# Router on plain normalised rows, and B's and C's products on both halves of the array's rows

## The chip, the cores and the metric

The kernel runs on one core of a Trainium2 chip. The metric is the device time of one execution in microseconds (us), as the median of several runs; the profiles are single executions taken by the hardware profiler. TensorE (PE) multiplies matrices, ScalarE (ACT), VectorE (DVE) and GpSimd (POOL) do the elementwise work, and SyncE (SP) issues the DMA transfers. PE reads from SBUF and writes to PSUM, which has eight banks.

## What is computed

The input is 8 sequences of 512 tokens with 128 features. Four blocks follow one another, each with a layer norm in front and a residual sum behind: a state-space mixer, a mixture of eight experts, a local attention with 16 heads, and the same mixture of experts again.

```python
x = x + mixer(_layernorm(x))
x = x + experts(_layernorm(x))
x = x + attention(_layernorm(x))
x = x + experts(_layernorm(x))
```

The change touches two places in it. In the mixer, after a short convolution gives `xb` (64 channels), one matrix of 24 rows gives three things:

```python
proj = jnp.einsum('blc,oc->blo', xb, W_xproj)
dt_raw = proj[..., :DTRANK]                       # 8 rows
b_raw = proj[..., DTRANK:DTRANK + DSTATE]         # 8 rows
c_raw = proj[..., DTRANK + DSTATE:]               # 8 rows
delta = jnp.clip(jax.nn.softplus(jnp.einsum('blr,cr->blc', dt_raw, W_dt) + b_dt), 0.0001, 1.0)
b_term = jnp.tanh(b_raw)
c_term = jnp.tanh(c_raw)
```

In the mixture of experts two small matrices (128 x 8 each) give the router's weights; every expert is computed for every token:

```python
router_probs = jax.nn.softmax(jnp.einsum('bsh,he->bse', x, w_router), axis=-1)
gate_weights = jax.nn.softmax(jnp.einsum('bsh,he->bse', x, w_gating) / GATE_TEMP, axis=-1)
g = jnp.einsum('bsh,ehf->ebsf', x, w_gate)
u = jnp.einsum('bsh,ehf->ebsf', x, w_up)
h = jax.nn.silu(g) * u
expert_out = jnp.einsum('ebsf,efh->ebsh', h, w_down)
cw = router_probs * gate_weights
```

## The kernel before

**The bulk of the work.** The experts' three products dominate. Weights and activations are kept as two halves, a rounded high half and the rest as the low half, and each product is three matmuls (high by high, low by high, high by low: `matmul3`, line 467), in the type `fp32r`. `ffn_stream` (line 1081) walks over the two expert blocks, the 8 sequences, the 8 experts and 4 slices of 128 hidden features, and issues a gate product `g`, an up product `u` and, some slices later, the down product `y`. In between, `hidden` (line 1162) runs on the other engines: silu on ACT, the product with `u` on DVE, the high half of `h` on ACT or DVE, the low half on POOL or DVE. The first sequence's first four experts are done in two halves of 256 tokens, so that the stream can begin before the mixer of sequence 0 has ended.

**The side work.** The mixer of the next sequences, the attention, the layer norms and the routers are written as Python generators ("lanes"). A planner (`Clock` and `Lanes`, lines 120 to 352) keeps a model clock for each engine, with a cost per operation (for PE in `product`, line 136), and at each step of the stream lets those lanes issue whose inputs would be there by that clock. The result is one fixed order of instructions for each engine: the engines run it in order and wait on semaphores. A changed cost or a changed operation early in the program therefore moves instructions everywhere behind it. Side work may hold at most 4 of the 8 PSUM banks once the stream runs (`sides`, line 404).

**Layer norm and halves.** `normalised` (line 515) is used by the mixer, the attention and the experts. `layernorm` makes the normalised rows `xn` (tokens on partitions, one buffer, which is a lane resource called "ln"). PE transposes them into a PSUM bank `tp`, ACT copies that to the high half `hi` (rounded), DVE subtracts to give the low half `lo`. "ln" is given back as soon as the transposes are issued.

**The router.** `ffn_prep` (line 980) calls `normalised` for a sequence (or for a half of sequence 0) and then multiplies the two router matrices (32 columns, `wr`) with both halves, read as plain fp32: for each half and for each of the four blocks of 128 tokens one matmul, which writes to its own 32 partitions of the bank `lps`. Lines 1001 to 1006. It appears in the profile as `lps_f<-xt_f,route`. What follows is small work on DVE, ACT, POOL and two PE transposes.

**dt, B and C.** `mamba_front` (line 604), for sequences 1 to 7, computes `xb` into the partitions 0 to 63 and once more into 64 to 127. The dt product (`wdt`, W_dt times the dt rows) takes the first 256 tokens through the rows 0 to 63 of the array and the last 256 through the rows 64 to 127, into two banks `mde`. B's and C's product is in `rows_bc` (line 654): one fp32 matmul with all 128 rows and 512 tokens, into a third bank `mbc`; the rows 64 to 127 of its weights `wbc` are zeros. The weights' 32 columns are repeated four times (line 585). Then ACT takes tanh of the bank to `bc` (rounded), tanh of the partitions 32 to 63 in place, and DVE subtracts to give the rounding's rest in these partitions. For sequence 0, `half` (line 685) does the same for each half of the tokens with 256 columns: first B's and C's product on all 128 rows, then dt's on one half of the rows. A program of filler products (`warm`) keeps PE running in the first 40 us.

An fp32 matmul appears in the profile as two PE records, an fp32r matmul as one.

## Time and profile before

| what | value |
|---|---|
| median of the 3 runs shown | 1381.18 us (1379.3 to 1381.27) |
| profiled execution, its own time | 1383.66 us |
| its span, first to last instruction | 1381.9 us |
| mean granted TensorE clock | 0.985 |
| PE busy, records | 1340.0 us, 10330 |
| DVE busy | 1041.4 us |
| ACT busy | 957.3 us |
| POOL busy | 942.5 us |
| the experts' three products on PE | 455.7, 455.6 and 450.1 us, 1584 records each |
| the router's product on PE | 11.6 us, 256 records |
| B's and C's product on PE | 9.7 us, 18 records |
| dt's product on PE | 7.0 us, 32 records |

A line of the profile names the engine, the operation, the tile that is written and those that are read, the shape, a count, and times; "idle before" with an arrow names what the engine waited for. Nearly all instructions are recorded under line 259, because a helper issues them, so they are told apart by their tiles. Groups of PE overlap in time: matmuls are pipelined, so a group's busy time is more than what it adds to the stream, and the distance between the starts of two groups that follow without a pause is what one costs.

### The profile page before, as it was taken

The page shows a single profiled execution, that of the slowest core. Times are in us where ns is not written, and L with a number is a line of the kernel's source. Part 1 is how long each engine was busy: PE and PEld are TensorE (multiplying, and loading weights), DVE is VectorE, ACT ScalarE, POOL GpSimd, SP SyncE. Part 2 cuts the span into 40 slices and gives each one's busy share as a digit, 9 for nine tenths or more (in the row PEclk, how much of TensorE's full clock was granted, in tenths as well). Part 3 has the DMA queues.
Part 4 walks back from the last instruction along what each step waited for, and adds up shares of the span by engine and source line. Part 5 has one row for each costly group of instructions (what it writes and reads, how often), then busy time and mean ns, then how long its engine had stood idle before and what let it go on. Part 6 is the DMA issues. An engine that isn't in the chain of part 4 may idle for free. (4 is left out here: it accounts for less than half of the span.)

```text
span 1381.9 us, 29693 instructions
## 1 busy us (share of the span) xinstructions
PE 1340.0 (97%) x10330; PEld 1058.3 (77%) x10330; DVE 1041.4 (75%) x3137; ACT 957.3 (69%) x1674; POOL 942.5 (68%) x1057
## 2 busy tenths in 40 slices
PE   7779999999999999999999999999999999999997
PEld 6667777777878877777777777777777777778786
DVE  6877888888888567878888788678787787774443
ACT  7558577776775557776786877767767768775654
POOL 4656676667667577767676758666666666777776
PEclk8889999999999999999999999999999999999999
DMA  3221123223221322343435444443534333413111
GB/s 124 73 64 49 53 54 88 57 62 92 62 62 39 71 65 56 78 103 87 107 86 117 99 94 96 95 101 77 125 97 96 81 92 72 102 36 89 40 39 38
DMA packets 230846, 107.75 MB, mean 78 GB/s; under 512 B 86402, under 2 KB 226601, under 8 KB 230697
## 3 DMA queue, kind: packets, MB, share of 16 engines
q1 hardware_dynamic: 230696, 105.87, 32.6%
q8 instruction: 81, 1.33, 0.4%
q14 instruction: 69, 0.56, 0.1%
HBM read 77.64 MB, written 27.79 MB: 76 GB/s over the span
## 5 line engine op out<-in xcount | busy, mean ns | idle before, releaser
L259 POOL TENSOR_TENSOR h<-h,h 128x512 fp32r<-128x512 f32 (+1 forms) x512 | 644.5, 1269 | 295.1 <-ACT h L259 232.0
L259 PE MATMUL u<-xt_f,wu 128*128 128x512 f32 (+1 forms) x1584 | 455.7, 396 | 9.5 <-ACT h L259 5.8
L259 PE MATMUL g<-xt_f,wg 128*128 128x512 f32 (+1 forms) x1584 | 455.6, 396 | 4.7 <-DVE mst L259 2.6
L259 PE MATMUL y<-h,wd 128*128 128x512 f32 (+1 forms) x1584 | 450.1, 394 | 3.2 <-POOL h L259 1.7
L259 DVE TENSOR_TENSOR h<-u,h 128x512 f32<-128x512 f32 (+1 forms) x438 | 292.9, 674 | 169.5 <-PE u L259 109.5
L259 ACT ACTIVATE h<-g 128x512 f32<-128x512 f32 (+1 forms) x528 | 305.5, 584 | 140.7 <-PE g L259 116.6
L259 ACT CAST h<-h 128x512 fp32r<-128x512 f32 (+1 forms) x447 | 267.6, 605 | 190.3 <-DVE h L259 188.9
L259 PEld LDWEIGHTS u<-xt_f,wu 128*128 128x128 f32 x1584 | 289.6, 190 | 79.8 <-ACT h L259 7.9
L259 PEld LDWEIGHTS g<-xt_f,wg 128*128 128x128 f32 x1584 | 290.4, 191 | 73.3 <-issue 3.9
L259 PEld LDWEIGHTS y<-h,wd 128*128 128x128 f32 x1584 | 290.7, 190 | 71.6 <-POOL h L259 2.4
L259 POOL TENSOR_TENSOR acc<-acc,cwb 128x512 f32<-128x512 f32 (+1 forms) x115 | 147.6, 1284 | 52.1 <-DVE cwb L259 28.8
L259 ACT ACT_TABLE_LOAD x112 | 143.7, 1283 | 31.2 <-PE g L259 29.7
L259 DVE CUSTOM_DVE_ANT_0 amasked<-as,maskq 128x60 f32<-128x60 f32 x640 | 95.3, 214 | 5.1 <-PE as L259 4.7
L259 DVE TENSOR_TENSOR cwb<-y,cwb 128x512 f32<-128x512 f32 (+1 forms) x115 | 77.3, 672 | 21.1 <-PE y L259 11.0
L259 DVE TENSOR_TENSOR apt<-aw,maskk 125x400 f32<-125x400 f32 (+2 forms) x160 | 87.9, 574 | 0.1
L259 DVE SCALAR_TENSOR_TENSOR h<-h,g 128x512 f32<-128x512 f32 (+1 forms) x90 | 58.2, 651 | 39.5 <-ACT h L259 38.4
L259 ACT ACTIVATE apt<-apt 125x400 f32<-125x400 f32 (+2 forms) x160 | 80.5, 541 | 0.4
L259 DVE SCALAR_TENSOR_TENSOR h<-u,h 128x512 f32<-128x512 f32 (+1 forms) x90 | 58.3, 653 | 4.0
L259 DVE DVE_READ_ACCUMULATOR2_ANT amx<- 128x1 f32 x640 | 52.9, 83 | 0.0
L259 DVE CAST h<-h 128x512 fp32r<-128x512 f32 (+1 forms) x81 | 46.4, 579 | 1.4
L259 PEld LDWEIGHTS ao<-apt,v 125*32 125x32 f32 (+2 forms) x1280 | 27.4, 109 | 14.7 <-issue 6.6
L259 DVE COPY v<-avr 125x128 f32<-125x128 f32 (+2 forms) x40 | 24.0, 600 | 17.7 <-PE ao L259 17.3
(195 smaller groups left out, 1234.0 us busy)
## 6 DMA issues: line engine op xcount, KB each, us to landing
cwb<-cwd_f SPq DMA_DIRECT2D x124, 256.0 KB
aqd<-apc SPq DMA_DIRECT2D x32, 192.0 KB
ks<-aqd SPq DMA_DIRECT2D x48, 93.8 KB
x_fo<-x SPq DMA_DIRECT2D x16, 256.0 KB
aqd<-apc SPq DMA_DIRECT2D x32, 128.0 KB
x_f<-x SPq DMA_DIRECT2D x15, 256.0 KB
qs<-aqd SPq DMA_DIRECT2D x48, 75.0 KB
aod<-aos SPq DMA_DIRECT2D x24, 100.0 KB
```

The costliest lines, as they stand in the source:

```text
L259: f(*args, **kw)
```

## The change

The router now reads the normalised rows as they are. `normalised` gets a switch `plain`, with which ACT copies the transposed rows a second time, unrounded, over the buffer `xn`, and `ffn_prep` multiplies that with one matmul for each block of 128 tokens. The buffer "ln" is given back after the router's products, no longer after the transposes, and the bank `tp` after both ACT's copy and DVE's subtraction.

B's and C's product for sequences 1 to 7 is split like dt's: 64 rows for each half of the tokens, into the second half of the same bank that holds dt's product of these tokens. So there are two banks `mde` and none `mbc`; tanh and subtraction come in two pieces each, and the banks are given back by the step that makes `delta`. `rows_bc` is gone. The weights `wbc` are written to both halves of the rows. For sequence 0, B's and C's product uses the rows 0 to 63 and dt's the rows 64 to 127, for both halves of the tokens.

```diff
-    def normalised(xc, tag, halves, nt=NT, give=True, quick=False):
+    def normalised(xc, tag, halves, nt=NT, give=True, quick=False, plain=False):
...
             e = pe.transpose(tp[:, t * P : (t + 1) * P], xn[:, t, :], ident)
-        lanes.give("ln", e)
+        if not plain:
+            lanes.give("ln", e)
         yield "A"
         hi, lo = halves()
         tp = tp[:, : nt * P]
-        act.copy(hi, tp)
+        e = act.copy(hi, tp)
+        if plain:
+            xn = xn.rearrange("p t d -> p (t d)")[:, : nt * P]
+            e = act.copy(xn, tp)
         yield "V"
-        freed(dve.tensor_tensor(lo, tp, hi.bitcast(F32), ALU.subtract))
+        freed(max(e, dve.tensor_tensor(lo, tp, hi.bitcast(F32), ALU.subtract)))
         yield "T"
-        return hi, lo
+        return (hi, lo, xn) if plain else (hi, lo)
...
-        pool.tensor_copy(
-            wbc.rearrange("p (c n) -> p c n", c=4), pa[:, None, A_PBC : A_PBC + 32].to_broadcast([P, 4, 32])
-        )
+        for h in range(2):
+            pool.tensor_copy(
+                wbc[INNER * h : INNER * h + INNER].rearrange("p (c n) -> p c n", c=4),
+                pa[:INNER, None, A_PBC : A_PBC + 32].to_broadcast([INNER, 4, 32]),
+            )
...
-        pde = yield from sides(*(([P, L // 2], f"mde{b}_{h}") for h in range(2)))
+        both = yield from sides(*(([P, 2, HALF], f"mde{b}_{h}") for h in range(2)))
+        for j, w in enumerate(("wdt", "wbc")):
+            for h in range(2):
+                hs = slice(INNER * h, INNER * h + INNER)
+                pe.matmul(both[h][:, j], consts[w][hs], xb[hs, h * HALF : (h + 1) * HALF], start=True, stop=True)
+        pde = [t[:, 0] for t in both]
+        yield "A"
+
+        bc = sb.tile([P, L], F32R, tag="bc", name=f"mbc{b}")
         for h in range(2):
-            hs = slice(INNER * h, INNER * h + INNER)
-            pe.matmul(pde[h], consts["wdt"][hs], xb[hs, h * L // 2 : (h + 1) * L // 2], start=True, stop=True)
-        bc, bc_there = yield from rows_bc(b, sb, consts, xb, L, second_act=lambda: act.activation(zb, v, AF.Silu))
+            act.activation(bc[:, h * HALF : (h + 1) * HALF], both[h][:, 1], AF.Tanh)
+        for h in range(2):
+            act.activation(both[h][32:64, 1], both[h][32:64, 1], AF.Tanh)
+        act.activation(zb, v, AF.Silu)
+        yield "V"
+        for h in range(2):
+            low = bc[32:64, h * HALF : (h + 1) * HALF]
+            bc_there = dve.tensor_tensor(low, both[h][32:64, 1], low.bitcast(F32), ALU.subtract)
         yield "V"
...
-    def rows_bc(b, sb, consts, xb, n, second_act=None, c=0):
...
-            pe.matmul(pbc, consts["wbc"], xb, start=True, stop=True)
-            pe.matmul(pde, consts["wdt"][hs], xb[hs], start=True, stop=True)
+            pe.matmul(pbc, consts["wbc"][:INNER], xb[:INNER], start=True, stop=True)
+            pe.matmul(pde, consts["wdt"][INNER:], xb[INNER:], start=True, stop=True)
...
-        xt = yield from normalised(xc, nm, halves, nt, t0 + nt == NT, quick=nt < NT)
+        *_, xf = yield from normalised(xc, nm, halves, nt, t0 + nt == NT, quick=nt < NT, plain=True)
...
-        for i in range(2):
-            for t in range(nt):
-                pe.matmul(
-                    lps[32 * t : 32 * t + 32], wr, xt[i][:, t * P : (t + 1) * P].bitcast(F32),
-                    start=(i == 0), stop=(i == 1),
-                )
+        for t in range(nt):
+            e = pe.matmul(lps[32 * t : 32 * t + 32], wr, xf[:, t * P : (t + 1) * P], start=True, stop=True)
+        lanes.give("ln", e)
```

More of the change, by code (lines that the diff above doesn't have):

```diff
@@ L652, in mamba_front @@
         handed[b] = xb, zb, delta, bc, bc_there, clock.end["A"] + LAGS["A"]
-    def rows_bc(b, sb, consts, xb, n, second_act=None, c=0):
-        pbc = (yield from side([P, L], f"mbc{b}_{c}"))[:, :n]
-        pe.matmul(pbc, consts["wbc"], xb, start=True, stop=True)
-        yield "A"
-        bc = sb.tile([P, L], F32R, tag="bc", name=f"mbc{b}_{c}")[:, :n]
-        act.activation(bc, pbc, AF.Tanh)
-        act.activation(pbc[32:64], pbc[32:64], AF.Tanh)
-        if second_act:
-            second_act()
-        yield "V"
-        there = freed(dve.tensor_tensor(bc[32:64], pbc[32:64], bc[32:64].bitcast(F32), ALU.subtract))
-        return bc, there
     def spread(dst, consts, bc, i, m):
@@ L706, in half @@
             pde, pbc = yield from sides(([P, HALF], f"mde0_{c}"), ([P, L], f"mbc0_{c}"))
-            hs = slice(INNER * c, INNER * c + INNER)
             pbc = pbc[:, :HALF]
-            pe.matmul(pbc, consts["wbc"], xb, start=True, stop=True)
-            pe.matmul(pde, consts["wdt"][hs], xb[hs], start=True, stop=True)
+            pe.matmul(pbc, consts["wbc"][:INNER], xb[:INNER], start=True, stop=True)
+            pe.matmul(pde, consts["wdt"][INNER:], xb[INNER:], start=True, stop=True)
             add[c](scanned(c, pbc, pde))
```

## The prediction

> **What bounds the kernel now.** I read the busy times by engine first. TensorE's row stands alone:

> ```profile
> PE 1340.0 (97%) x10330; PEld 1058.3 (77%) x10330; DVE 1041.4 (75%) x3137; ACT 957.3 (69%) x1674; POOL 942.5 (68%) x1057
> ```

> 97% is an average over stages, so the table by stretch comes next (columns: the stretch, its length, then busy us of PE, weight loads, DVE, ACT and POOL with their instruction counts, the granted clock, the DMA share, GB/s):

> ```profile
> 0.00:45.00 45.00, 33.31 (x188) 28.18 (x189) 30.87 (x65) 25.07 (x54) 20.98 (x28) 0.83 0.37 112
> 45.00:70.00 25.00, 21.02 (x131) 18.29 (x133) 18.94 (x57) 16.67 (x41) 17.93 (x28) 0.89 0.26 70
> 70.00:450.00 380.00, 365.69 (x1784) 291.80 (x1783) 316.46 (x603) 270.14 (x466) 254.09 (x264) 0.98 0.24 62
> 450.00:1200.00 750.00, 745.24 (x7269) 581.48 (x7268) 584.94 (x2222) 535.59 (x930) 517.44 (x619) 1.00 0.41 91
> 1200.00:1370.00 170.00, 170.00 (x944) 135.40 (x944) 87.71 (x189) 108.18 (x183) 127.03 (x117) 1.00 0.22 52
> ```

> Length minus PE's column is PE's idle time: 11.7 us in the first 45, 4.0 in the next 25, 14.3 up to 450, 4.8 up to 1200, none up to 1370. From 450 on PE's stream alone sets the time; before 450 it mostly does, with 30 us of waits; in the first 45 us a dependent chain through all engines does. So the change is priced in PE time first, and ACT, which receives work, is watched before 450 us. A PE group's cost in the stream is the distance from its start to the next group's start, since PE's ends are modelled.

> **The router.** The change takes its product from 16 PE records per sequence (two halves, four column groups, two records each) to 8. The timeline of PE shows both sizes: the usual 16, and, in the sequence near 1147 us where the second half came late, 8 by themselves:

> ```profile
> 1147.89 0.43 PE L259 MATMUL lps_f<-xt_f,route 128*32 128x128 f32 x8 [0.30 <-DVE xt_f L259]
> 1148.25 0.50 PE L259 MATMUL g<-xt_f,wg 128*128 128x512 f32 x1
> ...
> 1225.08 0.65 PE L259 MATMUL lps_f<-xt_f,route 128*32 128x128 f32 x16
> 1225.65 0.97 PE L259 MATMUL u<-xt_f,wu 128*128 128x512 f32 x3
> ```

> 16 records take 1225.65 - 1225.08 = 0.57 us, 8 take 0.36. That saves 0.21 us, in 15 full sequences and the second half of the first one (whose two column groups run beside each other, so as many waves go): 16 x 0.21 = 3.4 us. The first half's lies in the head.

> **B and C.** Per sequence from the second on (7), dt's product is 4 records of 64 rows and B/C's is 2 records of 128 rows x 512:

> ```profile
> 119.03 0.70 PE L259 MATMUL mde<-mxb,wdt 64*128 64x256 f32 x4
> 119.66 0.97 PE L259 MATMUL u<-xt_f,wu 128*128 128x512 f32 x3
> 120.46 1.02 PE L259 MATMUL mbc<-mxb,wbc 128*128 128x512 f32 x2
> 121.32 0.60 PE L259 MATMUL tp_f<-ident,xn_f 128*128 128x128 f32 x4
> ```

> dt costs 119.66 - 119.03 = 0.63 us, B/C 121.32 - 120.46 = 0.86 us, 0.43 per record. After, B/C is four more 64-row records on 256 columns, two in each row half, behind dt's. Half the columns is half of 0.43 per record, so two records in each half, the halves beside each other, cost 2 x 0.215 = 0.43 us. Upper end: they cost what dt's four cost with their switch of form, 0.63. Less than 0.43 is excluded, because the records of one half follow each other. I take 0.43, because the router's row shows added waves at their streaming price (0.21 for two of 128 columns). Saved: 0.86 - 0.43 = 0.43 each (lower end 0.23), x 7 = 3.0 us (1.6).

> **The head.** For the first half of sequence 0, dt's product stands behind B/C's on PE, 15.30 to 16.52 us, and DVE waits 2.49 us for it; B/C's subtraction, whose tanh was done at 16.17, queues behind that and starts at 17.08. With both products in different row halves dt is done about 1.1 us earlier. The planner puts 7 filler products instead of 5 in front of the next needed one (0.25 us each by the 1.23 us for 5), so 0.5 us remains, and ACT's wait of 1.78 us for the second half's B/C passes it on. Later, at 41.24, PE waits 2.36 us for DVE's low half; then the router's remaining 4 records (0.57) and three gate products (0.81) run. After, the router needs only ACT's new copy, and two of the three gate products need only the high half; both fit into that wait. Up to 0.57 + 0.54 less, but the next product needs DVE's 41.11 + 0.67 = 41.78, so 0.8 at most, and DVE, busy from 36.9 to 46 with short pauses, takes back part. I take 0.5 + 0.5 = 1.0 us for the head; ends 0 and 1.3.

> **What is added.** Router: one ACT copy of 128x512 from PSUM per sequence, 0.58 us as the cast beside it (mean 558 ns over 17 with two halves of 0.37): 15 x 0.58 + 2 x 0.37 = 9.4 us. B/C: two tanh become four, 4 x 0.38 (0.76 for two of 256 at 15.41) against 1.19 for two of 512 (at 69.99): 0.33 x 7 = 2.3 us. So 11.8 us more on ACT. DVE's subtraction of 0.68 becomes two of 0.42: 1.1 us. POOL copies B/C's weights as two halves instead of one of 0.287 us at 6.2, 8 us before use. No DMA is added (SP issues the same number); SP's queue sees some loads change places. Cover: ACT is idle 110 us between 70 and 450 and 214 between 450 and 1200. If the cover is gone the price is 11.8 us, at the lower end nothing. I take nothing, because PE's waits on ACT in the whole run are few:

> ```profile
> PE u L259 <- ACT h L259: 5.8, 3, 4.5
> PE mbx L259 <- DVE mst L259: 4.3, 2, 2.4
> PE g L259 <- DVE mst L259: 2.6, 1, 2.6
> ```

> (us, times, longest). The new wait of the router on ACT's copy has the expert stream queued behind it on PE; in the built order the router's products stand where they stood, after the low half's place, so by then the copy (ahead of the low half's subtraction) has been issued. The layer-norm buffer is held until the router's product, 3 to 8 us longer; once, near 184 us, a mixer's layer norm starts in that gap and comes 4 us later; dt's product of that front stands at 219.56. One PSUM bank per front is saved.

> [...]

> **Sum.** 3.4 + 3.0 + 1.0 = 7.4 us. The profiled execution's own time is 1383.66 us (span 1381.9); it becomes 1376.3. The median of the runs shown is 1381.18, 2.5 us less, so 1373.8. With the lower ends (1.6, head 0) 5.0 us: 1376.2; with head 1.3: 1373.5. The planner's clock sees the new costs and reorders everything after some 55 us, so waits before 450 move by a few us either way: own range 1371 to 1377.

> **Rivals.**
> 1. ACT takes the pace (slower). Place: the queue of ACT before `h`, where the copies and tanh stand. Price: all 11.8 us, gain 7.4: +4.4, 1385.6. It is slower by 0.2% when (7.4 + 2.8) / 11.8 = 86% of the added ACT time turns up as PE waits. For it: between 77 and 82 us PE stops 4.53 us behind ACT's table load and exponentials. Against: ACT's idle time, and after 450 PE waits only 4.8 us for anything.
> 2. The gain before 450 is eaten, because the next wait there ends when it ended before. Left: 10 routers after 450, 2.1 us: 1379.1. For it: 30 us of PE waits there. Against: they are few and long (9.5 of them between 77 and 92 us), and PE stood still for the router in only two of its 17 places (at 41.24 and 1147 us).
> 3. The new order shortens those waits of 77 to 92 us. In the built order two weight casts move ahead of that place on ACT, and DVE multiplies the first `h` before the last scan, not behind it. Half gone: 1373.8 - 4.8 = 1369.0.
> 4. It does not do what it says: the row halves do not overlap. Then 8 records of 0.215 and the switch (0.63 - 0.43 = 0.20) make 1.92 us against 1.49: 3.0 us lost instead of won, 3.4 + 1.0 - 3.0 = 1.4, 1379.8. Against: dt's four records, 0.63 us for what would be 0.86 in series.

> **The numbers.** Forecast 0.60, rival 1 0.10, rival 2 0.17, rival 3 0.10, rival 4 0.03. Within 0.2% (about what a measurement of this kernel can tell from no change) is 1378.4 to 1383.9: rivals 2 and 4 mostly, 0.19. Faster: forecast, rival 3 and a little of 2, 0.71. Slower: rival 1, 0.10. The range from 1368 to 1381 leaves out rival 1 and the edges.

> **What would show it.** In the profile after: the router in 8 records, 0.36 us to the next start; dt and B/C as one group of 8 records within 1.06 us (1.26 at the upper end, 1.92 for rival 4); the first gate product starting before 41 us; PE busy less by about 6 us; PE's waits behind ACT still near 6 us. The forecast is wrong if PE's waits between 45 and 450 us, 18.3 us now, grow by more than 4, and rival 3 holds if they shrink by as much.

## The result, and the profile after

The changed kernel takes 1399.7 us (median of 4 runs, 1395.56 to 1400.78), the kernel before 1380.24 us in the runs beside it: ratio 1.0135, interval 1.0112 to 1.0159. It is slower by 19 us where 7 us less was forecast. The profiled execution took 1400.08 us, its span is 1398.3 us.

First the busy times by engine, then the table by stretch of the kernel after (columns as in the prediction; the last stretch of 170 us, with no idle time in either, is left out):

```profile
PE 1344.8 (96%) x10218; PEld 1058.9 (76%) x10218; DVE 1049.5 (75%) x3133; ACT 969.9 (69%) x1728; POOL 941.1 (67%) x1052
```

```profile
0.00:45.00 45.00, 33.52 (x189) 29.36 (x190) 31.66 (x67) 25.34 (x55) 21.24 (x29) 0.84 0.37 112
45.00:70.00 25.00, 19.39 (x119) 16.68 (x118) 16.12 (x51) 15.41 (x37) 16.33 (x26) 0.91 0.27 78
70.00:450.00 380.00, 357.32 (x1681) 281.06 (x1680) 293.70 (x572) 264.29 (x479) 246.19 (x255) 0.97 0.22 58
450.00:1200.00 750.00, 743.23 (x7184) 580.23 (x7183) 607.21 (x2242) 543.75 (x953) 513.79 (x610) 1.00 0.43 92
```

PE has 112 records fewer and yet is busy 4.8 us longer, and between 45 and 450 us it is idle 5.6 + 22.7 = 28.3 us where it was 18.3. The forecast named its own refutation there (waits growing by more than 4). The added ACT time is as forecast (969.9 - 957.3 = 12.6 us), and DVE is not busier between 70 and 450 us but less busy, by 22.8 us: it stands still more, and 22.3 us of its work have moved behind 450 us.

The new products, in PE's timeline of the kernel after:

```profile
129.07 0.43 PE L259 MATMUL lps_f<-xn_f,route 128*32 128x128 f32 x8
129.42 0.97 PE L259 MATMUL g<-xt_f,wg 128*128 128x512 f32 x3
...
204.46 0.70 PE L259 MATMUL mde<-mxb,wdt 64*128 64x256 f32 x4
204.99 0.60 PE L259 MATMUL mde<-mxb,wbc 64*128 64x256 f32 x4
205.52 0.73 PE L259 MATMUL y<-h,wd 128*128 128x512 f32 x2
```

From start to next start the router costs 129.42 - 129.07 = 0.35 us, dt and B/C together 205.52 - 204.46 = 1.06 us. Both are the forecast's prices. So the loss is not in PE's products that were changed.

To see where it comes, I set the starts of the gate products (`g`, 1584 records in both) side by side. The first one starts 1.0 us earlier than before. The 481st, 437.0 us before, starts 12.0 us later (449.0), but there the side work is not level: the mixer's last spread product follows at 442.9 us before, and only at 490.9 after. The 553rd starts 16.6 us later, with the same mixer products behind it in both, and the end is 16.4 us later. I call the 553rd **the mark**: it splits the run into the stage that holds the mixers of later sequences, and the rest. Its line before, then after:

```profile
489.80 0.62 PE L259 MATMUL g<-xt_f,wg 128*128 128x512 f32 x2
```

```profile
506.36 0.63 PE L259 MATMUL g<-xt_f,wg 128*128 128x512 f32 x2
```

So the whole loss lies before the mark; from there to the end both kernels take the same (892.1 and 891.9 us). The two profiles are 16.4 us apart where the medians are 19.5, since the profiled execution of before took 1383.66 us.

What PE waits for between 45 and 450 us in the kernel after, costliest first, and DVE's waits between 45 and 460 us for the mixer's spread products, again after:

```profile
PE g L259 <- DVE mst L259: 4.7, 2, 4.5
PE u L259 <- ACT h L259: 4.1, 5, 2.1
PE u L259 <- DVE mst L259: 2.9, 3, 2.2
```

```profile
DVE mbx L259 <- PE mbx L259: 10.3, 12, 1.7
DVE mcc L259 <- PE mcc L259: 7.8, 7, 2.6
```

Before, DVE waited 3.4 us for `mbx` and 0.5 us for `mcc`:

```profile
DVE mbx L259 <- PE mbx L259: 3.4, 7, 1.0
DVE mcc L259 <- PE mcc L259: 0.5, 1, 0.5
```

With `macc`'s the sum of these waits is 4.4 us before and 20.2 us after: PE waits for DVE's scans `mst`, and DVE waits for PE's products of the mixer. One such place in the timeline of all engines, after:

```profile
152.17 1.21 DVE L259 TENSOR_TENSOR_SCAN mst<-mdec,mbx 128x512 f32<-128x512 f32 x1
...
153.43 1.62 PE L259 MATMUL u<-xt_f,wu 128*128 128x512 f32 x3 [2.20 <-DVE mst L259]
...
155.27 1.48 PE L259 MATMUL y<-h,wd 128*128 128x512 f32 x3
155.51 0.69 DVE L259 TENSOR_TENSOR macc<-mcc,mst 128x512 f32<-128x512 f32 x1 [1.76 <-PE mcc L259]
...
157.42 0.40 PE L259 MATMUL mbx<-mbc,sel 128*128 128x512 f32 x1
...
157.86 0.70 DVE L259 TENSOR_TENSOR mbx<-mbx,mxb 128x512 f32<-128x512 f32 x1 [1.66 <-PE mbx L259]
...
159.06 0.69 DVE L259 TENSOR_TENSOR h<-u,h 128x512 f32<-128x512 f32 x1
...
159.78 0.62 ACT L259 CAST h<-h 128x512 fp32r<-128x512 f32 x1 [6.42 <-DVE h L259]
159.80 0.96 PE L259 MATMUL g<-xt_f,wg 128*128 128x512 f32 x3 [1.28 <-DVE h L259]
```

PE stands 2.20 us for a bank that DVE's scan at 152.17 frees. Behind that in its queue stand the products `mcc` (154.85) and `mbx`, so DVE stands 1.76 us and 1.66 us for them. Behind its own `mbx` steps stands `h` (159.06), whose `u`, a product that started at 146.87, and whose silu, from 151.79 on, had long been there: ACT waits 6.42 us for it, and PE, 1.28 us, for the bank that it frees. Each engine works its queue in the program's order and holds what the other needs next. A second thing shows: the three `y` products at 155.27 take 1.48 us, where three at 149.67 take 0.86. The granted clock stands at 0.50 from 153.50 to 156.91 us. The stretch from 150 to 250 us before, then after:

```profile
150.00:250.00 100.00, 97.16 (x450) 75.63 (x450) 85.17 (x161) 70.55 (x114) 64.84 (x63) 1.00 0.28 74
```

```profile
150.00:250.00 100.00, 90.29 (x388) 69.32 (x387) 72.44 (x139) 61.94 (x110) 58.63 (x60) 0.95 0.22 60
```

6.9 us more idle, and 0.05 x 100 = 5 us lost at a lower granted clock. Over windows of 1 us from 45 to 250 us, the clock's shortfall sums to 15.0 us after and 9.6 us before. So by these windows 10.0 us of waits and 5.4 us of clock came on top. From the first gate product to the mark, from start to start, the kernel after takes 17.5 us more: 10.0 us of waits, 4.9 us of clock, and 2.6 us more for the products themselves at full clock, where the changed ones should have saved some 4. That the unchanged products cost several us more in the new sequence is measured; why, I have not found.

That is the trace's account. Whether the new order or the added work makes it had to be tried.

### The profile page after: what moved, and what is told of

It reads as the page before. It is cut to its first block, busy times and chain, and to the rows that moved or that the text cites. A ratio compares the mean times of both kernels' runs of the same rounds, so it can differ in the third digit from the quotient of the medians.

```text
span 1398.3 us, 29541 instructions
## 1 busy us (share of the span) xinstructions
PE 1344.8 (96%) x10218; PEld 1058.9 (76%) x10218; DVE 1049.5 (75%) x3133; ACT 969.9 (69%) x1728; POOL 941.1 (67%) x1052
## 5 line engine op out<-in xcount | busy, mean ns | idle before, releaser
L259 POOL TENSOR_TENSOR h<-h,h 128x512 fp32r<-128x512 f32 (+1 forms) x506 | 642.2, 1279 | 280.2 <-ACT h L259 216.5
L259 PE MATMUL g<-xt_f,wg 128*128 128x512 f32 (+1 forms) x1584 | 457.4, 397 | 12.0 <-DVE mst L259 6.7
L259 PE MATMUL u<-xt_f,wu 128*128 128x512 f32 (+1 forms) x1584 | 457.0, 397 | 11.4 <-ACT h L259 4.1
L259 PE MATMUL y<-h,wd 128*128 128x512 f32 (+1 forms) x1584 | 451.7, 395 | 4.7 <-POOL h L259 2.7
L259 DVE TENSOR_TENSOR h<-u,h 128x512 f32<-128x512 f32 (+1 forms) x430 | 286.6, 673 | 168.4 <-PE u L259 111.4
L259 ACT ACTIVATE h<-g 128x512 f32<-128x512 f32 (+1 forms) x528 | 305.4, 583 | 143.6 <-PE g L259 103.4
L259 ACT CAST h<-h 128x512 fp32r<-128x512 f32 (+1 forms) x455 | 272.3, 605 | 189.6 <-DVE h L259 188.5
L259 PEld LDWEIGHTS u<-xt_f,wu 128*128 128x128 f32 x1584 | 291.8, 191 | 83.7 <-ACT h L259 9.5
L259 PEld LDWEIGHTS g<-xt_f,wg 128*128 128x128 f32 x1584 | 290.3, 191 | 84.1 <-DVE mst L259 7.8
L259 PEld LDWEIGHTS y<-h,wd 128*128 128x128 f32 x1584 | 290.9, 190 | 74.7 <-POOL h L259 3.8
L259 POOL TENSOR_TENSOR acc<-acc,cwb 128x512 f32<-128x512 f32 (+1 forms) x115 | 146.8, 1276 | 65.4 <-DVE cwb L259 46.0
L259 DVE CUSTOM_DVE_ANT_0 amasked<-as,maskq 128x60 f32<-128x60 f32 x640 | 95.3, 214 | 5.8 <-PE as L259 5.8
L259 DVE SCALAR_TENSOR_TENSOR h<-h,g 128x512 f32<-128x512 f32 (+1 forms) x98 | 63.8, 654 | 42.1 <-ACT h L259 41.2
L259 DVE TENSOR_TENSOR cwb<-y,cwb 128x512 f32<-128x512 f32 (+1 forms) x115 | 77.4, 673 | 15.8 <-PE y L259 9.0
L259 DVE TENSOR_TENSOR apt<-aw,maskk 125x400 f32<-125x400 f32 (+2 forms) x160 | 88.6, 573 | 0.0
L259 ACT ACTIVATE apt<-apt 125x400 f32<-125x400 f32 (+2 forms) x160 | 81.7, 541 | 0.4
L259 DVE SCALAR_TENSOR_TENSOR h<-u,h 128x512 f32<-128x512 f32 (+1 forms) x98 | 63.9, 655 | 3.9
L259 DVE DVE_READ_ACCUMULATOR2_ANT amx<- 128x1 f32 x640 | 52.8, 82 | 0.0
L259 DVE CAST h<-h 128x512 fp32r<-128x512 f32 (+1 forms) x73 | 45.0, 618 | 1.2
L259 PEld LDWEIGHTS ao<-apt,v 125*32 125x32 f32 (+2 forms) x1280 | 27.5, 110 | 15.2 <-issue 7.8
L259 DVE COPY v<-avr 125x128 f32<-125x128 f32 (+2 forms) x40 | 27.4, 685 | 14.3 <-PE ao L259 14.0
```

What stands on the lines that cost most here:

```text
L259: f(*args, **kw)
```

## The experiments

Two devices recur. The planner decides the order by its own clock, so an edit that should not move anything charges that clock with the old call and issues the new one past it (`ghost` charges and issues nothing, `nc.` issues and charges nothing). And a constant of the planner changed by one or two thousandths of a us (a null change) gives another order of the same operations; the planner then also gives some steps to another engine (ACT's busy time is 957.3 us in before and 965.0 in n1, the first of them), so each engine's share is not quite the same.

**1. Is it the work or the order?** `e1_old_order` does all the change's work in the order of before (abridged):

```diff
+            nc.scalar.copy(xf, tp)                    # beside act.copy(hi, tp)
+        for t in range(nt):
+            nc.tensor.matmul(lps[...], wr, xf[...], start=True, stop=True)
-                pe.matmul(lps[...], wr, xt[i][...], ...)
+                pe.ghost("matmul", lps[...], wr, xt[i][...])
```

and the same for B and C. Its plain rows have a buffer of their own, so the layer norm's buffer is not held longer, as it is in the change. `e4_new_order` is its opposite: the order of after with the old products (`pe.ghost` for the new ones, no copy of the plain rows).

> All instructions of the change, in the order of the kernel before: the planner's clock is charged as if the old products, the old tanh pair and the old subtraction were issued, so every other instruction of the five engines stands where it stood before. The plain rows have a buffer of their own (the router's copied logits share it), and the small dt matrix lies in a buffer of xb to make room. Theory 'order' (the loss is the price of the changed order of all instructions, the changed instructions themselves do what the prediction priced): 1380.2 - 7.4 = about 1373 us, 1371 to 1377. Theory 'work' (the 11.8 us more on ACT, the split tanh and the new waits hold up the stream, in whatever order): 1390 us or more.

> The order of the changed kernel on every engine, with the products of the kernel before: the router on both halves in 16 records, no copy of the plain rows, B and C on all 128 rows (tanh still in four pieces). 'Order' (the 19 us are the new order's) says the time stays near the changed kernel's 1399.7 us or a little above it, since the dearer products return some 6.5 us to TensorE: 1396 to 1408. 'Work' (the added copies, tanh pieces and waits cost it) says about 1381, the time before.

Measured: e1 1380.78 us, ratio 0.9995 (0.998 to 1.0009); e4 1405.92 us, ratio 1.0174 (1.0149 to 1.0198). The whole 19 us follow the order, and 'work' is refuted twice. But e1 is not 1373 either, and misses 'order's 1371 to 1377: with nothing moved, the saving of 7 us does not arrive. In the order of after it does in part: e4, with the old products, is slower than after by some 5 us (by the ratios, interval about 1 to 10).

Where it went shows when e1's PE records are put beside before's one by one (the order is the same). The replaced groups give 6.9 us, which is the forecast's 7.4 nearly whole. PE's waits take back 2.3, and 2.4 are products that ran slower. The other 2.2 us stand in these two profiles, whose spans are 2.3 us apart (1379.6 and 1381.9), and not in the medians. The lead over before is 7.0 us at the gate product that before starts at 976.6 us, and 1.7 at 1189.8. PE at the place where most of it goes, e1's timeline and its stretches:

```profile
1142.58 0.43 PE L1033 MATMUL lps_f<-xf_f,route 128*32 128x128 f32 x8 [1.27 <-ACT xf_f L539]
```

```profile
1139.00:1143.00 4.00, 2.73 (x89) 1.96 (x87) 2.82 (x6) 3.97 (x8) 3.40 (x3) 1.00 0.49 55
1143.00:1147.00 4.00, 3.99 (x47) 2.80 (x47) 4.00 (x38) 3.80 (x6) 0.61 (x3) 0.63 0.10 32
1147.00:1151.00 4.00, 4.00 (x12) 2.98 (x11) 2.38 (x9) 1.53 (x4) 1.47 (x6) 0.51 0.66 120
```

and the same place before:

```profile
1143.00:1147.00 4.00, 3.25 (x84) 2.49 (x83) 3.32 (x6) 3.97 (x8) 3.40 (x4) 1.00 0.38 80
1147.00:1151.00 4.00, 3.37 (x61) 2.10 (x62) 3.85 (x37) 3.10 (x6) 0.94 (x2) 1.00 0.17 47
```

Before waits there as long, but in two pieces (0.91 and 0.30 us), and keeps its clock. In e1 one wait of 1.27 us is followed by 7 us at half speed, 3.4 us lost. So the saving is real in the products and was handed back where PE, earlier now, waits for what did not become earlier (here ACT's new copy). The clock's toll comes on top at this place; over the whole stream it is nearly level (12.3 us lost in e1, 11.5 in before), since e1 lost less before 450 us.

**2. One part at a time, planner live, and a null change.** `e2_router_alone` and `e3_bc_alone` take one half of the diff each. `n1_act` is the kernel before with

```diff
-            c = 0.1 + n / 1180
+            c = 0.102 + n / 1180
```

> The router's part alone, B and C as before, with the planner free to reorder. 'Work': 9.4 of the 11.8 us of added ACT time stand here, so most of the loss, 1394 to 1400 us. 'Order': the order moves nearly as much as with both parts (2841 of the lines of PE's order differ, with both parts 3042), so it can land anywhere from 1376 to 1400 us; near 1377 would say that this order is a good one.

> B's and C's part alone, the router as before, with the planner free. 'Work': 2.3 of 11.8 us of added ACT time against 3 us of saved PE time: 1380 us, within 3. 'Order': PE's order differs in only 649 lines, so a small move of either sign about 1377 us, 1373 to 1385.

> The kernel before with one number of the planner's clock changed: an ACT operation is charged 0.102 us fixed, not 0.100. No instruction is added or removed by the change itself, but the order changes (2782 lines of PE's differ), and with it some choices between two engines. 'Work': 1380 us, within 3. 'Order', in the form that the order before is better than its neighbours: 1385 to 1400 us. 'Order', in the form that just this change makes a bad order: 1380 us.

Measured: e2 1385.1 us (1.0025, 1.0014 to 1.0037), e3 1381.88 (1.0011, 0.9996 to 1.0026), n1 1388.63 (1.0066, 1.004 to 1.0091). Neither half costs 19 us, the two do not add up, and a change of no work at all costs 8 us. 'Work' fails on e2 and n1; e3 lies inside what both theories said and decides nothing.

**3. Is it a draw?** More changes of the planner's prices alone, in both kernels: `n2_before_dve` (DVE's fixed price 0.077 for 0.075), `n3_before_pe` (fp32r product 0.004 for 0.003), and on the changed kernel `a1_after_act`, `a2_after_dve` and `a4_after_priced`:

```diff
-            return n * 0.00053, "beside"
+            return n * (0.00084 if n > P else 0.00041), "beside"     # a4
```

> The changed kernel with the planner's fixed price of a ScalarE instruction at 0.102 instead of 0.100 us: the same work in another order (as with the kernel before, where this cost 8 us). 'Draw' (each order's waits are a draw, and the change only drew a bad one) says it leaves 1399.7 by several us, anywhere from 1378 to 1398. 'Worse as a kind' (the change leaves the planner a worse set of orders) says 1395 to 1405.

> The kernel before with the planner's fixed price of a VectorE instruction at 0.077 instead of 0.075 us: the same work in another order. 'Draw' (an order's waits are a draw, with a spread of some 10 us either way) says anywhere from 1374 to 1400. 'Settled' (the kernel before's order is nothing special, and n1 was a chance) says 1379 to 1384.

> The kernel before with the planner's fixed price of an fp32r product at 0.004 instead of 0.003 us: the same work in a third order. 'Draw' says anywhere from 1374 to 1400, 'settled' 1379 to 1384.

> The changed kernel with the same edit of the VectorE price. 'Draw' says anywhere from 1368 to 1394, that is, the spread of the kernel before's orders less the 6.5 us that the products save. 'Worse as a kind' says 1393 to 1405.

> The changed kernel with the planner's price of the products on half the array's rows set to what the profile shows (0.215 us for 256 columns, 0.052 for the router's 128 columns, where it reckons 0.136 and 0.068): the same work in an order that knows the true prices. 'Wrong prices' (the bad order came of the planner's mispricing of the new products) says this order is good: 1370 to 1380. 'Draw' says anywhere from 1368 to 1394.

Measured: a1 1376.51 us, ratio 0.996 (0.9948 to 0.9973); n2 1388.44 (1.0048, 1.003 to 1.0067); n3 1382.8 (1.0013, 0.9997 to 1.0029); a2 1381.4 (1.0006, 0.9993 to 1.002); a4 1391.42 (1.0078, 1.0051 to 1.0106). The changed kernel's work takes 1376.5 or 1399.7 us by 2% of one fixed price in the planner. 'Draw' holds on four of the five, and a1 came out 1.5 us better than its range; 'settled' fails on n2, while n3 fits both; 'worse as a kind' fails on a1 and a2; 'wrong prices' fails on a4: knowing the true prices gave a poor order. a1 is faster than both kernels.

**4. What in the changed kernel's order costs it?** First guess: DVE's queue has too much in it. `l1_before_no_clip` and `l2_after_no_clip` take 28 clips out of it, each in its own kernel's order:

```diff
-  decs["c", i] = dve.tensor_scalar(decs[i], decs[i], cap[:, i : i + 1], 1e-4, ALU.min, ALU.max)
+  decs["c", i] = dve.ghost("tensor_scalar", decs[i], decs[i], cap[:, i : i + 1], 1e-4, ALU.min, ALU.max)
```

> The kernel before, order kept, without the 28 clips of the mixer's decays on VectorE (the values of those decays are then not bounded): some 28 x 0.84 = 23 us less on VectorE between 45 and 460 us. Both theories: VectorE is late in a few places before too, so 1372 to 1380. It is the mate of the next kernel.

> The changed kernel, order kept, without the same 28 clips. 'Queue' (in the new order VectorE's queue holds the mixer's steps ahead of the products h that TensorE's banks wait for) says most of the 19 us goes: 1375 to 1387, within 8 us of its mate without the change. 'Elsewhere' (the loss is ScalarE's, a transfer's or the clock's own) says the distance to its mate stays 15 us or more: 1390 to 1399.

Measured: l1 1377.58 us, l2 1395.92 us. Each gains 3.8 us and the distance stays 18.3 (16.2 of it at the mark), as 'elsewhere' said. 'Queue', as I had put it, falls: the amount of DVE's work is not the loss. In l2 DVE's waits for `mbx` and `mcc` are 23.2 us, more than in after; DVE reaches the same wait sooner.

Second guess, from that: the lock-step itself. `l3_before_uncoupled`, `l4_after_uncoupled` and `l5_a1_uncoupled` let DVE's mixer steps read `mxb` in SBUF instead of the products:

```diff
-  bxs[i] = bx, dve.tensor_tensor(bx, bx, xb, ALU.mult)
+  nc.vector.tensor_tensor(st, xb, xb, ALU.mult)
+  bxs[i] = bx, dve.ghost("tensor_tensor", bx, bx, xb, ALU.mult)
```

> The kernel before, its order kept, with the mixer's steps on VectorE reading the rows mxb wherever they read TensorE's products mbx and mcc (the scan's input and the sum are then other values, and the products mbx and mcc are made but not read): as many instructions of the same size on VectorE, none of which waits for TensorE. 'Lock-step' and 'otherwise' both: VectorE waits only 4.4 us for those products here, so little changes: 1372 to 1381. It is the mate of the next kernel.

> The changed kernel, its order kept, with the same edit. 'Lock-step' (in this order VectorE stands still 20 us for mbx and mcc with products h queued behind, while TensorE stands for the banks that those steps free) says the distance to its mate falls from 19 us to at most 8: 1368 to 1385. 'Otherwise' (the waits for mbx and mcc lie beside others that end as late) says the distance stays 14 us or more: 1388 to 1398.

> The changed kernel in the order of the planner with 0.102 us for a ScalarE instruction (1376.5 us as it stands, VectorE waiting 7.3 us for mbx and mcc), with the same edit. 'Lock-step' says it gains little, 1369 to 1377, and that the changed kernel's two orders, 23 us apart as they stand, come within 8 us of each other. 'Otherwise' says they stay 15 us or more apart.

Measured: 1413.97, 1423.76 and 1409.86 us. The waits for the products are gone (0.4 us and none), but every kernel became slower, by 32, 24 and 33 us, and the steps themselves did; DVE's groups from 70 to 460 us (busy us, mean ns), before and l3:

```profile
L259 DVE TENSOR_TENSOR mbx<-mbx,mxb 128x512 f32<-128x512 f32 x28 | 19.4, 692 | 3.4 <-PE mbx L259 3.4
```

```profile
L862 DVE TENSOR_TENSOR mst<-mxb 128x512 f32<-128x512 f32 x28 | 28.5, 1017 | 0.1
```

The distances, 9.8 us between l4 and l3 and 13.9 between l4 and l5, are between what either theory asked for, and in kernels whose DVE steps cost more. Inconclusive.

Third: leave the work and its prices, and let the planner put a mixer step into DVE's queue only some time after it reckons the product to be there.

```diff
-                yield "V", e
+                yield "V", e + 0.4          # 0.8 in s8, 1.2 in s12
...
-            yield "V", max(there, e)
+            yield "V", max(there, e + 0.4)
```

> The changed kernel, same work, but the planner puts a mixer step into VectorE's queue only 0.4 us after it reckons the product mbx or mcc to be there. 'Lock-step' (VectorE's waits for those products, with h queued behind, are the loss): its waits for mbx and mcc fall from 20 to under 10 us and the time with them, to 1376 to 1391. 'Draw' (the time goes with no one wait): the time may fall or not, 1376 to 1402, whatever these waits do.

> The same with 0.8 us. 'Lock-step': waits for mbx and mcc under 8 us, 1376 to 1389. 'Draw': 1376 to 1402, whatever these waits do.

> The same with 1.2 us. 'Lock-step': waits for mbx and mcc under 8 us, 1376 to 1391 (the mixer may now come late itself). 'Draw': 1376 to 1402, whatever these waits do.

Measured: s4 1382.63 us (1.0001, 0.9986 to 1.0017), s8 1402.2 (1.0156, 1.0129 to 1.0182), s12 1391.08 (1.0064, 1.0043 to 1.0085). By total time s8 refutes 'lock-step' as it was put, and s12 sits on its edge; s8 is at the edge of 'draw' too. The mark tells more. Here are the kernels in full work, "mark" being the start of the 553rd gate product, "rest" the span from there to the end, "mixer wait" DVE's waits for the mixer's products between 45 and 460 us. Mark, rest and wait are of the one profiled execution, which for a1, s8 and e4 was 3 to 4 us faster than the median:

| kernel | median us | mark | rest | mixer wait |
|---|---|---|---|---|
| before | 1380.2 | 489.8 | 892.1 | 4.4 |
| n1, n2, n3 | 1388.6, 1388.4, 1382.8 | 487.0, 490.8, 489.6 | 898.6, 896.4, 892.0 | 8.5, 4.7, 9.2 |
| e1 | 1380.8 | 485.8 | 893.8 | 4.0 |
| after | 1399.7 | 506.4 | 891.9 | 20.2 |
| e4 (order of after) | 1405.9 | 508.5 | 892.7 | 21.2 |
| a1, a2, a4 | 1376.5, 1381.4, 1391.4 | 485.4, 488.3, 490.0 | 885.8, 893.6, 899.7 | 7.3, 6.7, 5.2 |
| s4, s8, s12 | 1382.6, 1402.2, 1391.1 | 488.0, 490.7, 496.0 | 892.1, 906.2, 890.9 | 3.5, 0.7, 1.9 |

With the slack the mixer wait goes, and the mark comes 10 to 18 us earlier than after's in all three; s4's clock from 150 to 250 us is back at 1.00 with 2.6 us idle, where after had 0.95 and 9.7. So two things make a total. Up to the mark, the one order with 20 us of mixer waits is the latest. The slack does not single those waits out: it makes a new order, and so do a1, a2 and a4, which do not aim at those waits and whose mark comes 16 to 21 us earlier, with 5 to 7 us of them. And s12, with 1.9 us of them, is still late by some 6 us. In the rest every order draws anew, 885.8 to 906.2 us, and s8 drew badly. Its PE waits in the attention stage:

```profile
979.85 0.50 PE L259 MATMUL aqk<-axt,wq_hi 128*128 128x512 f32 x1 [1.81 <-ACT axt L259]
...
983.60 0.74 PE L259 MATMUL aw<-qs,ks 51*127 51x102 bf16 x8 [1.57 <-DMA qs<-amts]
```

```profile
980.00:990.00 10.00, 7.67 (x132) 4.82 (x132) 6.55 (x45) 5.47 (x14) 3.71 (x9) 0.66 0.38 99
```

Nothing of the mixer's is in it: a short chain through ACT and a transfer is late, and the clock falls to 0.66 for 10 us.

## Why the prediction was wrong, point by point

- **Router, right.** 0.35 to 0.36 us in 8 records (one group of the kernel after, at 704.77 us, 0.43), 0.21 to 0.22 us saved each.
- **B and C, right.** 1.06 us for the group of 8, 0.43 saved each; the row halves do overlap (rival 4 is out). With the order held, the seven groups cost 10.4 us in e4 and 7.4 in after up to the mark: 2.9 saved, 3.0 forecast.
- **Head, right in size, not in its parts.** The first gate product starts at 40.8 us, 1.0 us earlier. The part from dt did not last: DVE's step behind that product comes 1.0 us earlier (15.55 for 16.56), its steps from 20 to 31 us 0.3, and those at 36 us 0.1. And the gate products did not fit into PE's wait of 2.36 us: they wait themselves, 2.04 us, for a scan of DVE that ends at 40.78. By 45 us the lead is 0.7. So the 1.0 is partly luck, and a weak sign: changes of the planner's prices alone put this start between 38.6 and 41.1 us.
- **The sum of the work, nearly right.** 7.4 us forecast; e1's replaced groups measure 6.9, of which 1.9 are sequence 0's, where 0.8 arrives at the first gate product (41.0 us).
- **ACT's added work hidden, right in the kernel after.** It is 12.6 us more, near the 11.8 forecast by chance: with the order held it is 6.7 (964.0 in e1), since these instructions overlap in part (in after a cast of 0.37 us at 37.33, the copy of 0.38 at 37.60), and the rest is work that the planner moved to ACT. PE's waits behind ACT between 45 and 460 us are 8.4 us after and 8.2 before. Rival 1 did not happen. In e1 one wait, the 1.27 us at 1142.58, is for the new copy.
- **The step that failed** stands in the paragraph of the sum: "The planner's clock sees the new costs and reorders everything after some 55 us, so waits before 450 move by a few us either way: own range 1371 to 1377." They moved by 10 us, with some 5 us of clock that the step did not have at all, and the unchanged products cost several us more in the new sequence, which it did not have either. Together they put the mark 16.6 us late, and the end 16.4. With no change of work the orders of before span 8 us (1380.2 to 1388.6), those of the changed kernel, with the three slacks, 26 (1376.5 to 1402.2). That spread was the largest term in the forecast's uncertainty, and it was priced at plus or minus 3.
- **Rival 2 (the gain is eaten by the next wait) holds in e1**, with its place wrong: not before 450 us, where the lead grew to 4 to 5 us, but between 970 and 1190. It was given 0.17.
- **Rival 3** looked at the one stall that the new order seemed to shorten. After has a 4.52 us wait at 84.45 us, and between 75 and 95 us PE is idle for 8.1 us where it was 9.5: it was not halved. Reading one place of the new order, and not the mixer's steps around 150 us, was the error of method: the changed order can be read without a run, and DVE's queue there for what stands behind `mbx` and `mcc`. That such a reading would have foretold the 16 us is not shown.

What is shown: the loss goes with the order (e1, e4) and arises before the mark, orders of equal work differ by more than the change is worth (n1 to n3, a1 to a4), and the amount of DVE's work is not the cause (l2). That the two queues in lock-step are how this order costs is read from the timeline and fits the late marks of after, e4 and l2, which share the order and its 20 to 23 us of mixer waits. It is not shown: the edit that should have isolated it (l4) made the steps themselves slower (the multiplication 0.96 us, 0.69 in before), and the slacks changed the whole order, which a1, a2 and a4 did with as much effect. Open is also whether the change leaves the planner worse orders on average: seven orders of the changed work average 1389.3 us, four of before 1385.0, with spreads far wider than that difference.

## What to carry to other kernels

Where a planner places every instruction by a model's clock, a change of prices is two changes: the work, whose products the profile prices to a few tenths of a us, and a new order, which is a draw; draw several orders of both kernels by null changes of a constant before a 0.5% edit is judged, and keep the best order. To price the work alone, hold the order and charge the planner the old costs; what of it arrives still depends on the order that is held (nothing in e1, some 5 us between e4 and after). When PE becomes earlier at a fixed order, look at the next place where it waits for a chain that did not become earlier: the gain can end there, and a drop of the clock can take more than the wait itself (3.4 us behind 1.27 in e1).

## What the runs showed of the hardware that I had not expected

**Half clock behind short waits.** In 17 profiles (all but l3 to l5), between 100 and 1330 us, PE's waits that began at full clock: of 13 of 2.1 us or more, 11 were followed within 5 us by the granted clock at 0.5; of 67 between 1.0 and 2.1 us, 19; of 51 between 0.7 and 1.0, four, each with a wait of 1.9 us that began 2.4 us after it. The low stretches there lasted 3.41 or 6.83 us (after: 0.50 from 153.50 to 156.91 and from 167.15 to 173.98), which at half speed is 1.7 or 3.4 us. So in these profiles a wait of 1.0 to 2.1 us cost itself and, in 19 of 67 cases, another 1.7 us or more.

**Where DVE's operands lie.** The mixer's multiplication took 0.69 us with one operand in PSUM (before) and 1.02 us with both, and its result, in SBUF (l3). The scan took 1.21 us in before and 1.72 us in l3, and GpSimd's own products of 128x512 slowed from 1.31 to 1.51 us. Why both engines slowed, no run here shows.
